# An expert's two products between the score products, and the first score of the unit behind ahead of the other steps: the order of one software-pipelined loop

## The chip, the core and the metric

The kernel runs on one core of one Trainium2 chip. The core's engines run side by side, each with its own instruction queue: TensorE (PE in the profile) multiplies matrices and writes into PSUM, VectorE (DVE) and ScalarE (ACT) read and write PSUM and SBUF, GpSimd (POOL) works on SBUF, and SyncE (SP) issues the transfers. The metric is the device time of one execution in microseconds. Three runs of the kernel before gave a median of 3007.34 us, from 3006.35 to 3009.61.

## What is computed

The reference is four blocks of attention and feed-forward network on 2048 tokens (16 sequences of 128, 256 features), each with a layer norm and a residual. The change is in the code of the last layer alone. Its attention has 16 heads of 16 features and lets every token attend to all 2048 context tokens; its feed-forward part is a mixture of eight experts, two of them weighted per token, plus a shared network of 352 hidden features:

```python
q, k, v = _fq_sym(q, axis=-1), _fq_sym(k, axis=-1), _fq_sym(v, axis=2)     # int8 grids
attn = jax.nn.softmax(jnp.einsum('bhqd,bhkd->bhqk', q, k), axis=-1)
out = jnp.einsum('bhqk,bhkd->bhqd', _fq_unsigned(attn, axis=-1), v)
...
combine = jnp.sum(jax.nn.one_hot(selected, E) * routing_weights[..., None], axis=1)   # top 2 of 8
g = jnp.einsum('nh,eih->nei', x, expert_gate)
u = jnp.einsum('nh,eih->nei', x, expert_up)
y = jnp.einsum('nei,ehi->neh', jax.nn.silu(g) * u, expert_down)
out = silu(g_sh) * u_sh @ shared_down.T + jnp.einsum('neh,ne->nh', y, combine)
```

The kernel treats the shared network as two more experts with a fixed weight, so each token passes ten experts of 176 features.

## The kernel before

**Units.** The method `l3` runs the last layer. Tokens are taken in 16 tiles of 128. A *unit* `u` is one head of one tile: tile `u // 16`, head `u % 16`; there are N = 256 units. For each unit the 128 x 2048 scores are made in four pieces of 128 x 512, each in a PSUM bank of its own: `scores` (L916, one matmul), `peak` (L922, VectorE's maximum of a piece), then `bias` (L927 and L928, two small VectorE operations over the four maxima), and `exponentials` (L938, four ScalarE activations that also sum, and one transposing transfer of the unit's result by SyncE, L942). `values` (L950, 16 small matmuls) uses the transposed result LAG = 4 units later.

**Steps.** All else in the layer is spread over the units as steps: a dictionary `steps` names, for an offset counted from the first unit of tile `t`, which functions run there. As offsets go past 16, steps of two or three tiles meet in one unit. Written by position (unit modulo 16), with the tile they serve left out:

- 0 and 1: layer norm of the next tile (`stats`, `norm`); 2 `turn_h` (two transposes on TensorE, one ScalarE copy); 3 `project_q` (four matmuls, then a VectorE addition, L984); 4 `quant_q` (three VectorE operations, then GpSimd), and `divide` (VectorE, L1017 to L1021, which frees the bank that the value products collect in); 5 `turn_o` (two transposes, two ScalarE operations); 6 `project_o` (four matmuls, then L1037 on VectorE); 7 `stats_m`, 8 `norm_m`, 9 `turn_m` (two transposes, one ScalarE copy); 10 `turn_q` (eight transposes in L1008, a ScalarE copy L1010 and a VectorE copy L1011); 11 `logits` (four small matmuls, a VectorE maximum, a ScalarE exponential L1062); 12 `top` and 13 `combine` (VectorE).
- 14, 15 and 0 to 7: one expert each, ten in all (`expert`, L1090 to L1103): four matmuls of 352 columns (two per half of the 256 features), two ScalarE activations out of that bank (L1095 `ma`, L1096 `mb`), and, as a returned function that is called later in the unit, L1099 on VectorE (`ma` times the gate half, out of the same bank), L1100 on GpSimd, and the return of the bank.
- 1, 4, 7 and 8: `turn_a` turns a part of the experts' results (four transposes, at 8 two; one ScalarE copy L973). 8, 9, 11 and 12: `down` (L1119, eight, eight, eight and four matmuls in the trace), which collects in a bank `moe` held from position 8 to 12.

**Order.** The loop is under a manual schedule: on every engine instructions run in the order in which they are written. The main part of one unit, L1156 to L1179, is:

```python
exponentials(u)
scores(u + 1, 2); peak(u + 1, 2); scores(u + 1, 3); peak(u + 1, 3)
bias(u + 1)
later = [f(t, u) for each step due]      # an expert's products and activations are in here
values(u - LAG)
scores(u + 2, 0); scores(u + 2, 1)
peak(u + 2, 0)
the functions in later                    # L1099 and L1100 of the expert
peak(u + 2, 1)
```

**Banks.** Seven PSUM banks `b0` to `b6` serve scores and steps; an eighth collects the value products. `take` (L904) gives out the free bank with the smallest number, `give` (L909) returns one with a number that says when in the unit it will be free: u + 0.2, 0.4, 0.6 and 0.8 for the four that the exponentials free, about u + 0.8 to u + 1.0 for a step's, u + 1.1 for an expert's. The choice is made when the program is built; on the chip the first instruction that writes into the bank waits for the last reader of what was in it. At the head of a unit six banks hold scores (four of `u`, two of `u + 1`), and the seventh is free or, at positions 9 to 12, holds `moe`.

Of the kernel before, what the change touches and what calls it, by code (L numbers as in the profile page):

```python
# [29 lines left out]
P = 128  # L30
NT = 16
D = 256
NH = 16
# [7 lines left out]
class Net:  # L41
# [841 lines left out]
    def l3(self, w3, moe_w):  # L883
# [7 lines left out]
        nc, tc = self.nc, self.tc  # L891
        qw, ow, qb, ob, kst, v, sv = (w3[n] for n in ("q", "o", "qb", "ob", "k", "v", "sv"))
        gate_w, wgu, wd = moe_w
        NE, IN = 10, 176
        LAG = 4
        E = mybir.EngineType
        with (tc.tile_pool(name="l3x", bufs=2) as pool, tc.tile_pool(name="l3p", bufs=3) as pp,
              tc.tile_pool(name="l3t", bufs=LAG + 1) as tp, tc.tile_pool(name="l3m", bufs=1) as mp,
              tc.tile_pool(name="l3e", bufs=3) as ep):
            st = {}  # L900
# [3 lines left out]
            def take(shape, name, dtype=F32):  # L904
                tag = min(banks, key=banks.get)
                del banks[tag]
                return self.bank(shape, tag, name, dtype), tag

            def give(tag, when):  # L909
                banks[tag] = when  # L910


            def scores(u, q):
                t, hd = divmod(u, NH)
                ps, tag = st["s", u, q] = take([P, 512], "piece")
                nc.tensor.matmul(ps, qTs[t % 2][:, hd, :],  # L916
                                 kst[q // 2][:, hd // 2, 512 * (q % 2):512 * (q % 2) + 512], start=True, stop=True)

            def peak(u, q):
                if q == 0:  # L920
                    st["nm", u] = self.s(4, "nm")
                nc.vector.tensor_reduce(st["nm", u][:, q:q + 1], st["s", u, q][0], AX.X, ALU.max, negate=True)  # L922

            def bias(u):
                t, hd = divmod(u, NH)
                nb = st["nb", u] = self.s(1, "nb")
                nc.vector.tensor_reduce(nb, st.pop(("nm", u)), AX.X, ALU.min)  # L927
                nc.vector.tensor_scalar(nb, nb, st["sq", t][:, hd:hd + 1], LN255, ALU.mult, ALU.add)  # L928

            def exponentials(u):  # L930
                t, hd = divmod(u, NH)
                if hd == 0:
                    st["z", t] = pool.tile([P, NH, 4], F32, name="z", tag="z")

                p, nb = pp.tile([P, T], I16, name="p", tag="p"), st.pop(("nb", u))
                for q in range(4):
                    ps, tag = st.pop(("s", u, q))
                    nc.scalar.activation(p[:, 512 * q:512 * q + 512], ps, AF.Exp, bias=nb,  # L938
                                         scale=st["sq", t][:, hd:hd + 1], accum_out=st["z", t][:, hd, q:q + 1])
                    give(tag, u + 0.2 * (q + 1))  # L940
                pT = st["pT", u] = tp.tile([P, NT, P], I16, name="pT", tag="pT")
                nc.sync.dma_start_transpose(pT, p)  # L942

            def values(u):
                t, hd = divmod(u, NH)
                if hd == 0:
                    st["av", t] = self.bank([P, NH, 16], "av", "av")
                pb = st.pop(("pT", u)).bitcast(F16)
                for c in range(NT):
                    nc.tensor.matmul(st["av", t][:, hd, :], pb[:, c, :], v[:, c, hd * 16:(hd + 1) * 16],  # L950
                                     start=(c == 0), stop=(c == NT - 1))
# [124 lines left out]
            def combine(t, u):  # L1076
# [10 lines left out]
                nc.gpsimd.memset(comb[:, 8:], 0.5)  # L1087
                st["comb"] = comb

            def expert(e):  # L1090
                def step(t, u):
                    ps, tag = take([P, 2 * IN], "gu")
                    self.matmul_acc(ps, [(st["mhT"][:, c, :], wgu[:, c, e, :]) for c in range(2)])
                    a, b = (ep.tile([P, IN], F32, name=n, tag=n) for n in ("ma", "mb"))
                    nc.scalar.activation(a, ps[:, :IN], AF.Tanh, scale=0.5)  # L1095
                    nc.scalar.activation(b, ps[:, IN:], AF.Identity, scale=st["comb"][:, e:e + 1])  # L1096

                    def rest():
                        nc.vector.scalar_tensor_tensor(a, a, 1.0, ps[:, :IN], ALU.add, ALU.mult)  # L1099
                        nc.gpsimd.tensor_tensor(act[:, e * IN:(e + 1) * IN], a, b, ALU.mult)  # L1100
                        give(tag, u + 1.1)
                    return rest
                return step  # L1103

            def turn_a(k):
                def step(t, u):
# [4 lines left out]
            def down(k):  # L1111
                def step(t, u):
# [7 lines left out]
                    if k == 3:  # L1120
# [6 lines left out]
            steps = {-16: [stats], -15: [norm], -14: [turn_h], -13: [project_q], -12: [quant_q], -6: [turn_q],  # L1127
                     20: [divide], 21: [turn_o], 22: [project_o],
                     23: [stats_m], 24: [norm_m], 25: [turn_m], 27: [logits], 28: [top], 29: [combine]}
            for e in range(NE):  # L1130
                steps.setdefault(30 + e, []).append(expert(e))
            for k, n in enumerate((33, 36, 39, 40)):
                steps.setdefault(n, []).append(turn_a(k))
            for k, n in enumerate((40, 41, 43, 44)):
# [2 lines left out]
            N = NT * NH  # L1137
# [4 lines left out]
            with tc.manual_schedule(engines={E.PE, E.DVE, E.Activation, E.Pool, E.SP}):  # L1142
                nc.gpsimd.memset(act[:, NE * IN:], 0.0)
                for qT in qTs:
                    nc.gpsimd.memset(qT, 0.0)
                for n in sorted(n for n in steps if n < 0):
                    for f in steps[n]:
                        f(0, -1)
                for q in range(4):
                    scores(0, q)  # L1150
                    peak(0, q)
                bias(0)
                for q in range(2):
                    scores(1, q)
                    peak(1, q)
                for u in range(N + 29):  # L1156
                    if u < N:
                        exponentials(u)
                    if u + 1 < N:
                        for q in (2, 3):  # L1160
                            scores(u + 1, q)
                            peak(u + 1, q)
                        bias(u + 1)
                    later = []
                    for t in range(NT):
                        for f in steps.get(u - NH * t, ()) if u - NH * t >= 0 or t > 0 else ():
                            later.append(f(t, u))
                    if 0 <= u - LAG < N:
                        values(u - LAG)
                    for q in range(2):  # L1170
                        if u + 2 < N:
                            scores(u + 2, q)
                    if u + 2 < N:
                        peak(u + 2, 0)
                    for f in later:
                        if f:
                            f()
                    if u + 2 < N:
                        peak(u + 2, 1)  # L1179


    def run(self):
# [79 lines left out]
```

## Time and profile before

| | |
|---|---|
| runs: median, lowest, highest | 3007.34, 3006.35, 3009.61 us |
| the profiled execution's own time | 3011.51 us |
| its span, first to last instruction | 3009.8 us |
| mean granted TensorE clock, share of full | 0.922 |
| busy over the span: PE, DVE, ACT, POOL | 82%, 65%, 58%, 33% |
| first exponential of unit 0, of unit 255 (start) | 1877.45, 2959.31 us |
| from a tile's first exponential to the next tile's, tiles 2 to 14 | 68.6 to 68.7 and 71.2 to 71.4 us in turn |

The last layer's loop takes the stretch from 1877 us to the end. Shares over the whole span mix it with three other layers, so the loop has to be read in its own stretch. The page that the profile prints has the busy time of each engine, groups of instructions by source line with the idle time ahead of them and what ended it, and transfers; further views give the same for a stretch, list who waited for whom, or put instructions in order of time. In a row of the last kind stand the start, the time from the first start to the last end of what is merged in the row, engine, line, operation, result and operands, shapes, the number of instructions, and in brackets the idle time ahead and its releaser. A TensorE row's end is modelled, and the loads of its weights stand apart as PEld.

### The profile page before, as it was taken

How to read it: one execution, taken by the hardware profiler on the slowest of the kernel's cores; microseconds unless marked ns; L12 is line 12 of the kernel's file. 1: busy time of each engine (PE TensorE's matmuls, PEld its weight loads, DVE VectorE, ACT ScalarE, POOL GpSimd, SP SyncE). 2: the span in 40 equal slices, each digit the busy share in tenths (PEclk: the TensorE clock that was granted, in tenths of full speed). 3: DMA queues.
4: the chain of work that ended last, by engine and by line, in shares of the span. 5: the costliest groups of instructions: out<-in, count | busy, mean ns of one | idle time of the engine just before them, and what ended most of it. 6: DMA issues, size and time to landing. Idle time of an engine off the chain costs nothing. (4 is left out here: it accounts for less than half of the span.)

```text
span 3009.8 us, 41685 instructions
## 1 busy us (share of the span) xinstructions
PE 2460.5 (82%) x14066; PEld 1556.2 (52%) x14066; DVE 1956.3 (65%) x5041; ACT 1755.0 (58%) x4636; POOL 1000.7 (33%) x1587
## 2 busy tenths in 40 slices
PE   4789999999999875888888885777777777777778
PEld 2456666666666543456555653344444444444445
DVE  2455666666665434566666653887788787878784
ACT  1234444444444332555555541998888888888885
POOL 2344444444443322555555541111111111112111
PEclk9899999999999887999999997589899898989999
DMA  5000000000000003000000002876666666666673
GB/s 205 1 1 1 1 1 1 1 1 1 1 1 1 1 28 102 6 3 5 5 5 4 3 1 72 154 135 123 124 117 128 121 124 121 126 122 125 118 128 62
DMA packets 559830, 171.38 MB, mean 57 GB/s; under 512 B 538912, under 2 KB 555904, under 8 KB 558848
## 3 DMA queue, kind: packets, MB, share of 16 engines
q1 hardware_dynamic: 559616, 168.72, 27.8%
q8 instruction: 111, 1.82, 0.2%
q14 instruction: 103, 0.84, 0.1%
HBM read 32.37 MB, written 2.10 MB: 11 GB/s over the span
## 5 line engine op out<-in xcount | busy, mean ns | idle before, releaser
L938 ACT ACTIVATE p<-piece,nb,hs 128x512 int16<-128x512 f32 x1024 | 785.2, 791 | 27.4 <-issue 17.0
L922 DVE TENSOR_REDUCE nm<-piece 128x1 f32<-128x512 f32 x1024 | 652.1, 684 | 107.7 <-PE piece L916 99.8
L916 PE MATMUL piece<-kst,qT 128*128 128x512 bf16 x1024 | 366.5, 414 | 200.6 <-DVE ma L1099 89.6
L1100 POOL TENSOR_TENSOR act<-ma,mb 128x176 f32<-128x176 f32 x160 | 89.0, 558 | 765.1 <-DVE ma L1099 764.7
L233 PE MATMUL gu<-w_L_ffn_wgu,mhT 128*128 128x352 f32 x640 | 252.5, 523 | 11.6 <-ACT p L938 8.0
L225 ACT COPY pT<-tp 128x512 f32<-128x512 f32 (+1 forms) x208 | 116.6, 563 | 201.6 <-PE tp L209 200.1
L916 PEld LDWEIGHTS <-qT 128*128 128x128 bf16 x1024 | 77.4, 99 | 297.2 <-issue 168.8
L938 ACT ACTIVATION_READ_ACCUMULATOR p<-piece,nb,hs 128x1 f32 x1024 | 222.2, 217 | 0.0
L259 POOL TENSOR_TENSOR kx<-kT,hmask 128x512 f32<-128x512 f32 x128 | 132.8, 1043 | 190.4 <-PE scores L262 125.4
L264 DVE TENSOR_REDUCE mx<-scores 128x4 f32<-128x512 f32 x128 | 88.2, 689 | 161.3 <-PE scores L262 161.0
L233 PEld LDWEIGHTS gu<-w_L_ffn_wgu,mhT 128*128 128x128 f32 x640 | 122.7, 205 | 131.4 <-ACT p L938 83.5
L950 PEld LDWEIGHTS <-pT 128*128 128x128 f16 x4096 | 144.7, 99 | 82.6 <-issue 68.0
L278 PEld LDWEIGHTS av<-v,pT 128*128 128x128 f32 x1024 | 136.2, 201 | 78.2 <-ACT pT L225 66.6
L233 PE MATMUL gu<-w_L_ffn_wgu,hT 128*128 128x352 f32 x512 | 173.7, 461 | 2.1 <-DVE act L432 1.6
L524 ACT ACTIVATE s<-s,nb,qs 128x128 f32<-128x128 f32 x256 | 123.2, 482 | 87.2 <-DVE nb L522 87.2
L278 PE MATMUL av<-v,pT 128*128 128x17 f32 x1024 | 136.3, 265 | 41.0 <-ACT pT L225 41.0
L269 ACT ACTIVATE p<-scores,mx,qs 128x128 f32<-128x128 f32 x256 | 96.9, 459 | 118.8 <-DVE mx L267 111.0
L950 PE MATMUL av<-v_int,pT 128*128 128x16 bf16 x4096 | 143.7, 171 | 19.6 <-DVE o L1021 19.6
L262 PE MATMUL scores<-kx,qT 128*128 128x512 f32 x256 | 153.0, 682 | 2.3 <-ACT qT L225 1.8
L539 PE MATMUL oproj<-w_L_ffn_oT,oT 128*128 128x256 f32 x512 | 128.9, 396 | 3.7 <-ACT oT L533 3.6
L1119 PE MATMUL moe<-w_L_ffn_wd,aT 128*128 128x256 f32 x448 | 127.7, 434 | 3.6 <-ACT p L938 3.6
L233 PE MATMUL q<-w_L_ffn_qT,hT 128*128 128x512 f32 x256 | 127.9, 600 | 2.1 <-DVE rot L478 2.0
(362 smaller groups left out, 5305.7 us busy)
## 6 DMA issues: line engine op xcount, KB each, us to landing
pT<-p SPq DMA_TRANSPOSE x256, 4.3
w_L_ffn_wgu<-in_L_ffn_wgu SPq DMA_DIRECT2D x1, 3520.0 KB, 11.6
w_L_ffn_wgu<-in_L_ffn_wgu SPq DMA_DIRECT2D x1, 2816.0 KB, 12.7
x<-in_x SPq DMA_DIRECT2D x16, 128.0 KB, 4.5
ctxT<-in_ctxT SPq DMA_DIRECT2D x4, 512.0 KB, 5.2
w_L_ffn_qT<-in_L_ffn_qT SPq DMA_DIRECT2D x1, 2048.0 KB, 7.9
w_L_ffn_oT<-in_L_ffn_oT SPq DMA_DIRECT2D x1, 2048.0 KB, 15.6
ctx<-in_ctx SPq DMA_DIRECT2D x16, 128.0 KB, 2.0
```

The costliest lines, as they stand in the source:

```text
L225: nc.scalar.copy(out[:, j0:j0 + m, :], ps)
L233: self.nc.tensor.matmul(ps, a, b, start=(j == 0), stop=(j == n - 1))
L259: nc.gpsimd.tensor_tensor(kx, kT[oc].unsqueeze(1).to_broadcast([P, 4, P]), self.hmask[:, hs].unsqueeze(2).to_broadcast([P, 4, P]), ALU.mult)
L262: nc.tensor.matmul(ps, qT[:, oc, :], kx, start=True, stop=True)
L278: nc.tensor.matmul(av[:, 4 * g + h, :], pT[:, h, :], v[:, 4 * g + h, :], start=True, stop=True)
L524: nc.scalar.activation(s[:, j, :], s[:, j, :], AF.Exp, bias=nb[:, j:j + 1], scale=qs[:, j:j + 1], accum_out=z[:, j:j + 1])
L539: nc.tensor.matmul(proj, oT[:, j, :], w["o"][:, c, :], start=(c == 0), stop=(c == 15))
L916: nc.tensor.matmul(ps, qTs[t % 2][:, hd, :], kst[q // 2][:, hd // 2, 512 * (q % 2):512 * (q % 2) + 512], start=True, stop=True)
L922: nc.vector.tensor_reduce(st["nm", u][:, q:q + 1], st["s", u, q][0], AX.X, ALU.max, negate=True)
L938: nc.scalar.activation(p[:, 512 * q:512 * q + 512], ps, AF.Exp, bias=nb, scale=st["sq", t][:, hd:hd + 1], accum_out=st["z", t][:, hd, q:q ...
L950: nc.tensor.matmul(st["av", t][:, hd, :], pb[:, c, :], v[:, c, hd * 16:(hd + 1) * 16], start=(c == 0), stop=(c == NT - 1))
L1119: nc.tensor.matmul(ps, st["aT", k][:r, j, :], wd[:r, c, :], start=(c == 0), stop=(c == 13))
```

## The change

An expert no longer has one function for products and activations. `expert` returns two: `product(c)`, one of the two halves of the products (the first takes the bank), and `activations(u)`, which issues the two ScalarE operations and returns the function with L1099 and L1100 as before. The experts leave the dictionary `steps` and stand in one of their own, `experts`. The loop's order changes for all units:

- between the scores (u + 1, 2) and (u + 1, 3) stands product 0 of the unit's expert, if there is one, and after (u + 1, 3) product 1;
- each peak is written right behind its score (new helper `score`);
- the score (u + 2, 0) and its peak stand behind `bias(u + 1)`, ahead of the activations, the steps and `values`;
- the score (u + 2, 1) and its peak stand at the very end, behind the functions in `later`. On TensorE, where these functions have no instruction, that is the place behind `values` as before.

The steps, their positions, the numbers given to `give` and all shapes stay as they are.

```diff
             def expert(e):
-                def step(t, u):
-                    ps, tag = take([P, 2 * IN], "gu")
-                    self.matmul_acc(ps, [(st["mhT"][:, c, :], wgu[:, c, e, :]) for c in range(2)])
+                def product(c):
+                    if c == 0:
+                        st["gu"] = take([P, 2 * IN], "gu")
+                    nc.tensor.matmul(st["gu"][0], st["mhT"][:, c, :], wgu[:, c, e, :], start=(c == 0), stop=(c == 1))
+
+                def activations(u):
+                    ps, tag = st["gu"]
                     a, b = (ep.tile([P, IN], F32, name=n, tag=n) for n in ("ma", "mb"))
...
-                return step
+                return product, activations
...
-            for e in range(NE):
-                steps.setdefault(30 + e, []).append(expert(e))
+            experts = {30 + e: expert(e) for e in range(NE)}
...
+                def score(u, q):
+                    if u < N:
+                        scores(u, q)
+                        peak(u, q)
+
                 for u in range(N + 29):
+                    now = [experts[u - NH * t] for t in range(NT) if u - NH * t in experts]
                     if u < N:
                         exponentials(u)
+                    for c in range(2):
+                        score(u + 1, 2 + c)
+                        for product, _ in now:
+                            product(c)
                     if u + 1 < N:
-                        for q in (2, 3):
-                            scores(u + 1, q)
-                            peak(u + 1, q)
                         bias(u + 1)
-                    later = []
+                    score(u + 2, 0)
+                    later = [activations(u) for _, activations in now]
                     for t in range(NT):
                         for f in steps.get(u - NH * t, ()) if u - NH * t >= 0 or t > 0 else ():
-                            later.append(f(t, u))
+                            f(t, u)
                     if 0 <= u - LAG < N:
                         values(u - LAG)
-                    for q in range(2):
-                        if u + 2 < N:
-                            scores(u + 2, q)
-                    if u + 2 < N:
-                        peak(u + 2, 0)
                     for f in later:
-                        if f:
-                            f()
-                    if u + 2 < N:
-                        peak(u + 2, 1)
+                        f()
+                    score(u + 2, 1)
```

## The prediction, made before the changed kernel ran

> **What bounds the kernel now.** I read the loop's stretch in four views: the stretch's busy times, its waits by engine, the groups of ScalarE by line, and the instructions in order of time over one tile's sixteen units. First the stretch from 1980 to 2940 us, in which nearly fourteen tiles pass in the steady pattern (columns: stretch, its length, busy time of PE, weight loads, DVE, ACT, POOL, clock, DMA):
>
> ```profile
> core 0: us, PE busy (x) PEld busy (x) DVE busy (x) ACT busy (x) POOL busy (x), PEclk, DMA share, GB/s
> 1980.00:2940.00 960.00, 746.59 (x5884) 433.53 (x5883) 765.42 (x1869) 818.71 (x2195) 165.80 (x313) 0.92 0.67 124
> ```
>
> ScalarE works 819 of 960 us, more than any other engine, and its instructions run in one fixed order. So the loop's length is ScalarE's work plus what ScalarE waits. Its waits in the same stretch, total and times:
>
> ```profile
> ACT ma L1095 <- PE gu L233: 60.6, 60, 2.2
> ACT gp L1062 <- DVE gnm L1060: 39.8, 13, 3.5
> ACT mhT L973 <- PE tp L971: 17.0, 14, 1.2
> ACT p L938 <- issue: 13.4, 13, 1.0
> ```
>
> Half of the wait is for an expert's products; the rest stands at three places without an expert. The order of time, over positions 8 to 11 of a tile (position = unit modulo 16), shows which bank each TensorE step waited for:
>
> ```profile
> 2445.52 0.81 ACT L938 ACTIVATE p<-piece,nb,hs 128x512 int16<-128x512 f32 x1
> 2445.71 1.99 PE L1119 MATMUL moe<-w_L_ffn_wd,aT 128*128 128x256 f32 x8 [0.26 <-ACT p L938]
> ...
> 2448.80 1.89 PE L1119 MATMUL moe<-w_L_ffn_wd,aT 128*128 128x256 f32 x8
> ...
> 2450.95 0.37 ACT L973 COPY mhT<-tp 128x256 f32<-128x256 f32 x1 [1.22 <-PE tp L971]
> 2451.37 0.78 ACT L938 ACTIVATE p<-piece,nb,hs 128x512 int16<-128x512 f32 x1
> ...
> 2453.65 0.78 ACT L938 ACTIVATE p<-piece,nb,hs 128x512 int16<-128x512 f32 x1
> 2453.81 0.61 PE L1008 MATMUL htp<-identb,qi 128*128 128x128 bf16 x8 [0.38 <-ACT p L938]
> ...
> 2454.45 1.01 ACT L1010 COPY qT<-htp 64x1024 bf16<-64x1024 bf16 x1
> ...
> 2457.42 3.25 PE L1119 MATMUL moe<-w_L_ffn_wd,aT 128*128 128x256 f32 x8
> ...
> 2461.25 0.27 ACT L1062 ACTIVATE gp<-logits,gnm 128x8 f32<-128x8 f32 x1 [2.75 <-DVE gnm L1060]
> ```
>
> Exponentials start every 0.76 us. With E for the start of a unit's first, TensorE gets the four banks they free at E+0.92, 1.68, 2.44 and 3.20 (first score after E=2451.37 at 2452.29, the next at 2453.05, the transposes at 2453.81). The transposes of position 10 stand on the third bank, and their copy follows the fourth exponential (2453.65 + 0.80) without a gap.
>
> [...]four gu matmuls take 1.45 us at some places and 2.55 or 2.71 at others, and tiles alternate between about 68.7 and 71.3 us. [...]here the q weight loads begin at 2423.66 and their matmuls at 2423.96. [...]here DVE's copy of qT waits for ScalarE's 15 times, 12.7 us.
>
> **The change, part by part.** Sums are per tile, relative to E, at full clock unless said. Durations: score 0.21 after the one before and 0.42 until DVE can start; one product 0.66 (half of 1.45, less the tail; +0.13 at the end); peak 0.62; bias pair 0.33; L1099 0.25 to the next; ScalarE's ma at E+3.23, mb +0.22, next unit +0.29, thus 3.74 for an expert unit without a stall.
>
> *The weave.* Which bank a step gets follows from the order of takes. Now: first score the spare bank, product pair the second freed (1.68), ready at 1.68+1.45+0.1 = 3.23, just when ma wants it: no slack. After: product 0 takes the first freed (0.92 to 1.58), the score the second (1.68), product 1 from 1.89, ready at 2.78. Slack 0.45. But the spare bank is freed by L1099 of the unit before, so this slack covers only its lateness up to about 0.8.
>
> *First score behind in front of the steps.* DVE now does this peak before a step's operations, not after. At positions 3 and 6 (q and o projections) the DVE addition waits for TensorE and today peak and L1099 stand behind it: L1099 runs at the next E+1.52 (2426.24 against 2424.72). After: q in the fourth bank 3.20 to 4.22, addition to 4.66, L1099 at once: next E+0.92. Then first score 1.31, products 1.52 to 3.18, ready 3.27 instead of 3.87. The stall of 0.64 at positions 4 and 7 goes. What is late next is their four transposes: fourth bank, after the score, 3.26 to 3.86, copy at 3.90 instead of 3.78: 0.12. Length 4.77 to 4.36: -0.41, twice.
>
> Position 5: L1099 before it sits behind 2.13 us of DVE steps of position 4 (division and quantisation). The sum on DVE is unchanged, bias to L1099; I get E+2.0 as today (1.98) and a stall of 1.1: +0.1.
>
> Positions 14 and 15: products start one bank earlier and L1099 runs about 0.4 earlier. Slow-clock gu at 14: ready 3.9 instead of 4.5, -0.55. In the other tiles, where 15 is slow: -0.5. I take -0.55.
>
> *The price.* The early score takes the bank that steps used. A step that takes a bank now gets the fourth (3.20) instead of the third (2.44). In expert units ma and mb cover it: ScalarE's copy is due at 3.74, two transposes end at 3.58; four end at 3.80, so position 1 pays 0.1. Without an expert the copy is due at 3.08, and nothing covers:
>
> - Position 8: moe gets the fourth bank, so L1119's eight matmuls start at 3.20, not 2.47. TensorE is then full until the transposes of position 9: from 2445.71 to 2450.95 it is 5.24 us, with the same number of scores in between (four). mhT comes 0.72 later; its stall goes from 1.22 to 1.95. +0.72.
> - Position 10: transposes at 3.20, end at 3.81, copy at 3.85 instead of 3.08. +0.77. The score that follows waits for DVE's half of that copy as today (next E+0.85).
> - Position 11: the score at 2.44 now stands before L1119's eight matmuls and the logits behind them. Today they start at 2.06; after, at 2.44 plus 0.21 (0.38 on slow clock): 2.65 to 2.85. +0.75, bounds 0.6 and 0.8 while their clock stays as it is.
>
> Positions 12 and 13: DVE works through from bias to bias; the sum stays, 0.
>
> Scores, products, activations, transfers and L1100 are the same in number; the transposing transfer is issued at the same place behind the exponentials and its queue passes nothing; values run four units later and stay covered. DVE's bias comes at 3.2 in an expert unit, before the next exponential at 3.74. That cover is 0.5.
>
> Sum per tile: -0.41 -0.41 -0.55 +0.1 +0.1 +0.72 +0.77 +0.75 = +1.07. Thirteen full tiles (2 to 14): 13.9. Tile 15 has no q transposes and no q projection: about +0.7. Tile 1 has a spare bank; only its logits stand behind one score more: +0.5. Units after 255 have no scores: 0. Sum +15 us. The profiled execution took 3011.5 us (span 3009.8), 4.2 over the median of the runs: 3011.5+15 = 3026.5 there, 3022 as a median.
>
> **The rivals.** *Clock against it.* [...] If each tile becomes like the long ones, 1.3 us per tile (half of 71.3-68.7) come on top: 17 us, 3039. For it: the gap on TensorE before L1119 at 11 grows by about 1.5 us. Against: two tiles now make 139.95 us, 41 windows of 3.413, and a new length locks elsewhere.
>
> *Not slower: the clock pays it back.* One mechanism: fewer half-rate windows. The long tiles lose 2.15-1.05 at position 5, 0.75 at 11 and the rest at 15 to them. If all tiles become like the short ones, -1.3 per tile meets +1.07: -3 us, 3004; it decides once the stalls at 5 and 11 no longer alternate. For it: products that start at 0.92 split the idle stretch of TensorE in an expert unit; even locking to the present length would give no change. Against: 10 and 11 get emptier.
>
> *Faster: the bank is not what the steps wait for.* If the fourth bank were ready when the third is, the losses of 2.24 at 9, 10 and 11 fall away and -1.17 per tile stays: -16 us, 2991. Against: L1119 and the transposes start within 0.2 of an exponential's release in the rows above. For it only that the three places could shift against each other. An even larger gain, all 60.6 us of ma's wait, would need position 5 without its stall, which DVE's sum denies.
>
> **How the numbers follow.** This kernel's runs tell 0.2% (6 us) from no change: below 3001.3 is faster, above 3013.4 slower. Forecast 3022, 0.48, own range 3014 to 3032 (losses of 1.9 to 2.4, gains of 1.0 to 1.6 per tile, and a locking of the length within 0.4). Clock against it 0.12. Clock pays it back 0.22, mostly within 0.2% (0.16), 0.04 faster, 0.02 slower. Bank not the limit 0.18, all faster. Faster 0.22, same 0.16, slower 0.62. The range for 8 in 10 runs from the low part of the clock case to just over the long-tile case: 2999 to 3041.
>
> **What would show it.** In the profile after: ma's wait for gu falls from 60.6 us to about 40; a new wait of the qT copy for the htp transposes, 0.77 each; mhT's wait rises from 1.22 to near 1.95 each, gp's from about 3.1 to 3.8; L1119's first eight start at the fourth exponential's release. The transposes of qT still starting at E+2.44 would refute the price; position 4 still above 4.7 us would refute the gain; ma's wait gone at position 5 would refute DVE's sum.

## The result, and the profile after

The changed kernel takes 3035.91 us (median of 4 runs, 3032.51 to 3038.6) against 3006.85 us (4 runs) of the kernel before: ratio 1.0099, 95% interval 1.008 to 1.0119. It is 29 us slower. The profiled execution took 3036.77 us, its span 3035.1 us against 3009.8. Of the 25.3 us between the two spans, 1.7 lie ahead of the loop's first exponential, where the change touches nothing, 2.1 in tiles 0 and 1, 18.7 in the thirteen tiles 2 to 14, 2.8 in tile 15, and nothing behind the last exponential.

The loop's stretch after, again nearly fourteen tiles (columns: stretch, length, busy time of PE, weight loads, DVE, ACT, POOL, clock, DMA):

```profile
core 0: us, PE busy (x) PEld busy (x) DVE busy (x) ACT busy (x) POOL busy (x), PEclk, DMA share, GB/s
1980.00:2965.00 985.00, 777.24 (x5940) 455.06 (x5940) 779.60 (x1887) 822.42 (x2213) 164.52 (x313) 0.89 0.67 121
```

ScalarE does the same work as before (822 against 819 us) in 985 instead of 960 us, and TensorE's clock is down from 0.92 to 0.89. ScalarE's waits in it:

```profile
ACT ma L1100 <- PE gu L1095: 46.0, 53, 2.3
ACT gp L1062 <- DVE gnm L1060: 44.6, 13, 3.7
ACT mhT L973 <- PE tp L971: 28.9, 14, 3.2
ACT p L938 <- issue: 23.7, 13, 2.1
ACT qT L1010 <- PE htp L1008: 9.4, 13, 1.1
ACT aT L973 <- PE tp L971: 4.5, 15, 0.3
```

The wait for the products fell by 14.6 us. All else rose: mhT by 11.9, the exponentials by 10.3, gp by 4.8, and two waits are new, qT's and aT's. Where they come from is seen in the order of time, positions 8 to 10 of a tile (L1095 is now the line of the products; behind it line numbers are five higher than before, so L1100 is L1095 of before and L1124 is L1119):

```profile
2455.13 0.79 ACT L938 ACTIVATE p<-piece,nb,hs 128x512 int16<-128x512 f32 x1
...
2456.06 1.99 PE L1124 MATMUL moe<-w_L_ffn_wd,aT 128*128 128x256 f32 x8 [0.26 <-ACT p L938]
...
2459.16 1.89 PE L1124 MATMUL moe<-w_L_ffn_wd,aT 128*128 128x256 f32 x8
...
2461.30 0.37 ACT L973 COPY mhT<-tp 128x256 f32<-128x256 f32 x1 [1.98 <-PE tp L971]
...
2461.57 0.79 ACT L938 ACTIVATE p<-piece,nb,hs 128x512 int16<-128x512 f32 x1
...
2464.02 0.38 PE L916 MATMUL piece<-kst,qT 128*128 128x512 bf16 x1 [0.38 <-ACT p L938]
...
2464.78 0.61 PE L1008 MATMUL htp<-identb,qi 128*128 128x128 bf16 x8 [0.38 <-ACT p L938]
...
2465.42 1.01 ACT L1010 COPY qT<-htp 64x1024 bf16<-64x1024 bf16 x1 [0.69 <-PE htp L1008]
```

The early score runs at 2464.02, 2.45 us after the unit's first exponential: it has the third bank. The transposes for qT run at 3.21 us, the release of the fourth, and moe's first matmuls at position 8 too (2456.06 is 0.93 after the fourth exponential's start). Each ScalarE operation behind them waits.

These waits are not yet the 29 us, for the gains stand against them. The granted clock in the two traces is either full or half. Of the half-rate stretches in their clock records, 73 before and 85 after, 38 and 54 last 3.413 us, and all others but the very last (2.10 and 1.76 us) last 2 to 18 times that; a window below is 3.413 us. In tiles 3 to 14 there are 3.5 such half-rate windows per tile before and 4.75 after. Two neighbouring tiles of the kernel before, the first with two half-rate windows (at positions 11 and 14), the second with five:

```profile
2129.18:2197.85 68.67, 52.75 (x430) 30.88 (x428) 55.55 (x136) 59.34 (x160) 12.20 (x23) 0.95 0.66 122
2197.85:2269.12 71.27, 56.08 (x430) 32.40 (x428) 55.80 (x136) 59.44 (x160) 12.24 (x23) 0.88 0.65 123
```

and two of the changed kernel, again with two (at the same positions) and with five:

```profile
2134.70:2203.24 68.54, 53.34 (x429) 31.28 (x428) 56.03 (x137) 59.05 (x160) 12.12 (x23) 0.95 0.70 125
2203.24:2274.94 71.70, 56.48 (x429) 33.27 (x428) 56.23 (x137) 59.16 (x161) 12.11 (x23) 0.88 0.67 120
```

With the same number of these windows a tile is no longer than before, or 0.4 us longer. Before, the two kinds take turns; after, of the tiles 3 to 14 all but the first of these two have five.

### The profile page after: what moved, and what is told of

Its sections match the earlier page's. It is cut to its first block, busy times and chain, and to the rows that moved or that the text cites. A ratio compares the mean times of both kernels' runs of the same rounds, so it can differ in the third digit from the quotient of the medians.

```text
span 3035.1 us, 41685 instructions
## 1 busy us (share of the span) xinstructions
PE 2490.6 (82%) x14066; PEld 1575.2 (52%) x14066; DVE 1964.9 (65%) x5041; ACT 1752.3 (58%) x4636; POOL 999.5 (33%) x1587
## 5 line engine op out<-in xcount | busy, mean ns | idle before, releaser
L922 DVE TENSOR_REDUCE nm<-piece 128x1 f32<-128x512 f32 x1024 | 670.8, 684 | 120.9 <-PE piece L916 114.6
L916 PE MATMUL piece<-kst,qT 128*128 128x512 bf16 x1024 | 404.2, 432 | 136.4 <-ACT p L938 50.7
L1095 PE MATMUL gu<-w_L_ffn_wgu,mhT 128*128 128x352 f32 x640 | 274.7, 520 | 37.5 <-ACT p L938 37.3
L916 PEld LDWEIGHTS <-qT 128*128 128x128 bf16 x1024 | 99.3, 103 | 250.2 <-issue 148.8
L1095 PEld LDWEIGHTS gu<-w_L_ffn_wgu,mhT 128*128 128x128 f32 x640 | 124.9, 208 | 128.3 <-ACT p L938 73.5
L1124 PE MATMUL moe<-w_L_ffn_wd,aT 128*128 128x256 f32 x448 | 137.6, 459 | 3.4 <-ACT p L938 3.4
```

Source lines behind the costliest of these rows:

```text
L916: nc.tensor.matmul(ps, qTs[t % 2][:, hd, :], kst[q // 2][:, hd // 2, 512 * (q % 2):512 * (q % 2) + 512], start=True, stop=True)
L1095: nc.tensor.matmul(st["gu"][0], st["mhT"][:, c, :], wgu[:, c, e, :], start=(c == 0), stop=(c == 1))
L1124: nc.tensor.matmul(ps, st["aT", k][:r, j, :], wd[:r, c, :], start=(c == 0), stop=(c == 13))
```

## The experiments

Theory A: the early score costs, since it takes the third freed bank and leaves a step the fourth; the weave gains. Rival B: the weave, or what it does to TensorE's clock, costs, and the banks don't matter. All changes below are made to the changed kernel unless said. Lengths of a position are the distance from a unit's first exponential to the next unit's, means over tiles 3 to 14, read off ScalarE's instructions in order of time:

| position | before | after | difference forecast | measured | weave alone | early score in expert units only |
|---|---|---|---|---|---|---|
| 0 | 3.73 | 3.51 | 0 | -0.22 | 3.55 | 3.51 |
| 1 | 4.20 | 4.52 | +0.1 | +0.32 | 4.11 | 4.50 |
| 2 | 4.01 | 3.95 | 0 | -0.06 | 3.77 | 3.95 |
| 3 and 4 | 8.55 | 8.08 | -0.41 | -0.47 | 8.17 | 8.08 |
| 5 | 5.76 | 6.22 | +0.1 | +0.46 | 5.65 | 5.98 |
| 6 and 7 | 8.52 | 8.13 | -0.41 | -0.39 | 8.10 | 8.14 |
| 9 | 4.84 | 5.53 | +0.72 | +0.69 | 4.84 | 5.22 |
| 10 | 3.99 | 4.79 | +0.77 | +0.80 | 3.99 | 3.99 |
| 11 | 6.50 | 6.89 | +0.75 | +0.39 | 5.28 | 5.26 |
| 13 | 4.18 | 5.04 | 0 | +0.86 | 4.17 | 4.17 |
| 14 and 15 | 9.10 | 8.16 | -0.55 | -0.94 | 8.31 | 8.10 |
| whole tile | 69.97 | 71.41 | +1.07 | +1.44 | 66.55 | 67.50 |
| half-rate windows in it | 3.5 | 4.75 | | +1.25 | 1.8 | 2.4 |

(Positions 8 and 12 stay at 3.29 and 3.30.)

**The weave alone.**

```diff
-                    score(u + 2, 0)
                     later = [activations(u) for _, activations in now]
...
+                    for q in range(2):
+                        if u + 2 < N:
+                            scores(u + 2, q)
+                    if u + 2 < N:
+                        peak(u + 2, 0)
                     for f in later:
                         f()
-                    score(u + 2, 1)
+                    if u + 2 < N:
+                        peak(u + 2, 1)
```

> The weave alone; the first score of the unit behind goes back behind the values, so the steps get the third bank again. Theory A (the early score costs, because steps get the fourth bank; the weave gains): positions 8 to 13 return to the lengths of before (9: 4.84, 10: 3.99, 11: 6.1 to 6.9, 13: 4.18 us), expert units without a step keep 3.51; positions 4 and 7 return to about 4.77. Some 1.5 us per tile under the kernel before: about 2986 us. Rival B (the weave is what costs, through TensorE's clock): stays near 3036 us.

Measured: 2970.46 us (4 runs), ratio to before 0.9869, interval 0.9853 to 0.9885. Its ScalarE waits over a like number of tiles:

```profile
ACT ma L1100 <- PE gu L1095: 44.2, 54, 2.8
ACT gp L1062 <- DVE gnm L1060: 23.7, 13, 3.5
ACT mhT L973 <- PE tp L971: 15.8, 13, 1.2
ACT p L938 <- issue: 13.3, 13, 1.0
```

mhT's, qT's and the exponentials' waits are those of before; the products' wait is as low as in the changed kernel. Rival B falls: the weave gains, more than theory A forecast, since gp's wait fell too (position 11 at 4.6 in most tiles), although nothing there was changed. That is the clock: it is at 0.932, and a tile has 1.8 half-rate windows instead of 3.5.

**The early score alone**, with both products behind it.

```diff
                     for c in range(2):
                         score(u + 1, 2 + c)
-                        for product, _ in now:
-                            product(c)
...
                     score(u + 2, 0)
+                    for product, _ in now:
+                        for c in range(2):
+                            product(c)
```

> The early score alone, products together behind it. Theory A: the products now get the bank of the third exponential (2.44 us after the unit's first), are ready at 4.0 and ma, due at 3.0, waits 1.0 us in each of the ten expert units, on top of the losses at 8 to 13: some 10 us per tile over the weave's, about 3125 us. Rival B: without the weave near 3007 us, as before.

Measured: 3159.98 us (6 runs), ratio 1.0494, 1.0476 to 1.0512. The products' wait is 0.84 us in each of the ten expert units where the clock is up and mostly about 2.1 where it is down. A tile has 8.4 half-rate windows, and what the products' wait exceeds 0.84 us by comes to 71 us in tiles 2 to 14 of the profiled execution (3174.89 us, clock 0.885, one of the slower ones). So the slow clock is more than enough for the miss of 35 us. The 0.84 us is the price of the third bank, paid ten times a tile.

**The early score in expert units only.**

```diff
-                    score(u + 2, 0)
+                    early = bool(now)
+                    if early:
+                        score(u + 2, 0)
```

(otherwise the order at the end is that of before)

> Weave, and the early score only in units with an expert; positions 8 to 13 in the old order. Theory A: 8 to 13 as before, experts as in the changed kernel: 67.2 us per tile with a full clock at positions 5 and 11, 69.2 with a slow one, against 69.98 before and 71.68 after: 2970 to 2996 us. Rival B: the order at 8 to 13 is not what costs, near 3036 us.

Measured: 2981.34 us (4 runs), ratio 0.9905, 0.9888 to 0.9921. So the early score at the positions without an expert costs 3035.9 - 2981.3 = 54.6 us. In expert units it costs 2981.3 - 2970.5 = 10.9 us more than the weave alone: positions 1 and 2 grow by 0.4 and 0.2, for the copies now wait for the fourth bank, and 3, 4, 6 and 7 gain 0.05 in sum. Another 0.4 at position 9 and 0.3 at position 5 are slow clock: 9 is 4.82 us in nine of the twelve tiles and about 6.4 in three, where a half-rate window falls on 8 and 9.

**Position 12 alone in the old order.**

```diff
+                    early = u % NH != 12
```

(the rest as in the run before this one)

> The changed kernel with the old order at position 12 alone. Theory A: moe's last four matmuls start at 1.9 instead of 2.8 us, VectorE's addition behind them no longer waits 0.95, and the gap ahead of position 14 falls from 2.06 to 1.03 us; positions 9 to 11 stay at 5.43, 4.76 and 7.0. If the clock's pattern stays, 1.03 per tile less: 3022 us. Rival B: no gain at 14, near 3036 us.

Measured: 3013.02 us (20 runs), ratio 1.0015, 1.0007 to 1.0024. The gap ahead of position 14 is back at 1.02 us in every tile. In the changed kernel the order of time there is:

```profile
2475.78 0.58 PE L916 MATMUL piece<-kst,qT 128*128 128x512 bf16 x1 [0.38 <-ACT p L938]
...
2476.16 1.91 PE L1124 MATMUL moe<-w_L_ffn_wd,aT 128*128 128x256 f32 x4
...
2478.11 0.42 DVE L1126 TENSOR_TENSOR x<-moe,x 128x256 f32<-128x256 f32 x1 [0.95 <-PE moe L1124]
...
2481.87 0.78 ACT L938 ACTIVATE p<-piece,nb,hs 128x512 int16<-128x512 f32 x1 [2.06 <-issue]
```

moe's last four matmuls stand behind the early score and run at half rate, 1.91 us instead of 1.03; VectorE, which works without a break up to the next bias, waits 0.95 for them, and the exponential of position 14 is that much later. The order alone doesn't do it: tiles 2 to 4 of the changed kernel have the same order but no half-rate window there, the four matmuls take 1.03 us, and position 13 is 4.17 us as before. In this run no such window falls on position 12, so it doesn't tell whether the old order would have covered slow matmuls. The gain of 23 us is more than this term alone (0.86 x 13 = 11): the slow clock at positions 5 and 11 went in part as well.

**Position 10 alone in the old order**, the same edit with 10 for 12.

> The changed kernel with the old order at position 10 alone. Theory A: the copy of qT no longer waits, position 10 falls from 4.76 to 3.99 us, and position 9 stays at 5.43; by this term alone 10 us, 3026 us, and more or less where the clock's windows fall otherwise. If qT's wait is not from the order at this position: 4.76 us stays.

Measured: 3002.41 us (20 runs), ratio 0.9997, 0.9985 to 1.0009. Position 10 is back at 4.00 to 4.14 us in tiles 2 to 13, 9 stays at 5.43 in all but one. The term is confirmed; the time fell by 33 us where the term is worth 10. Undoing either position also takes half-rate windows away (3.25 per tile with the old order at 12, 3.8 here, 4.75 in the changed kernel), so these two times don't price the terms. The lengths do, in tiles with the same windows.

**More work for TensorE at positions 10 to 13**, in the changed kernel and in the kernel before: the value products are made again, into the same place.

```diff
                     if 0 <= u - LAG < N:
-                        values(u - LAG)
+                        pb = st["pT", u - LAG]
+                        for _ in range({10: 3, 11: 2, 12: 3, 13: 3}.get(u % NH, 1)):
+                            st["pT", u - LAG] = pb
+                            values(u - LAG)
```

> The changed kernel, with the value products of positions 10, 12 and 13 made three times and of 11 twice into the same place, so that TensorE has more to do where it is emptiest; the result stays. If this keeps the clock up, position 11 falls from 7.0 to about 5.0 us, the gap ahead of 14 from 2.06 to 1.03, and 5 may fall from 6.4 to 5.2, while 9 (5.43) and 10 (4.76), which theory A puts down to the banks alone, stay: 67 to 68 us per tile, 2970 to 2986 us. If the clock is only a consequence and not a cost, or the extra work doesn't reach it: near 3036 us.

> The kernel before with the same extra value products. With the clock up: position 11 from 6.1 and 6.9 to 4.6 us, 14 and 15 to 4.2 and 3.7, 5 at 5.2: 66.4 us per tile, about 2957 us. What the change costs without the clock is then the difference to the other run of this kind: theory A, banks and order alone, some +0.5 us per tile (+7 us); if the clock was the only cost, 0.

Measured: 2999.59 us (20 runs), 0.9979 (0.9969 to 0.9989), for the changed kernel; 2986.98 us (5 runs), 0.9939 (0.9918 to 0.996), for the one before. Both gain from work that nothing needs, so the clock is a cost. It is not the only one: positions 9 and 10 stay at 5.43 and 4.76, and the changed kernel stays behind, by 0.4% instead of 1.0% (0.9979 over 0.9939; the two intervals above don't overlap). The separation isn't clean: one half-rate window per tile is left in most tiles of either kernel, in the changed one at 11, which stayed at 6.2, in the one before at position 5 (6.8 us in most tiles). The clock is not quite the same (0.933 to 0.938 in the runs of the changed kernel, 0.936 to 0.941 in those of the one before), so the 0.4% may have clock in it too. And the profiled executions don't stand for the medians, 2989.52 us being 10 below and 2998.38 us 11 above theirs: in them the last tiles are 68.26 and 68.23 us long, all but equal.

**L1099 ahead of VectorE's steps**, on the weave alone.

```diff
+                            if f in (project_q, project_o, quant_q):
+                                while later:
+                                    later.pop(0)()
                             f(t, u)
```

> The weave alone, and L1099 of the expert ahead of the q and o additions (positions 3 and 6) and ahead of the quantisation (4) on VectorE, so that the spare bank comes free earlier. If the stalls at 4, 7 and 5 are the late L1099: position 4 from 4.63 to 4.0, 7 from 4.59 to 4.0, 5 from 5.42 to about 4.5 us, some 2 us per tile, 2942 us. If they are something else: 2970 us as with the weave alone.

Measured: 2949.05 us (4 runs), ratio 0.9809, 0.9782 to 0.9836: the fastest kernel here but for the next, whose interval overlaps it. Position 4 is 4.10, 5 is 4.83, 7 is 4.01, so the stalls there were L1099's lateness. ScalarE's wait for the products fell from 44.2 to

```profile
ACT ma L1100 <- PE gu L1095: 14.4, 15, 1.0
ACT ma L1100 <- POOL q L997: 5.6, 13, 0.5
```

The second line is what is left at position 5, put down to GpSimd. The prediction held that the sum of VectorE's work there denies the unit without its stall; the sum is the same here, and only the order was in the way.

**The two together.**

> The weave with L1099 ahead of the VectorE steps, and the extra value products at positions 10 to 13. If the rest of position 11's and 14's wait is the slow clock: 11 from 5.68 to 4.62, 14 from 4.66 to 4.2, against 0.28 lost at 12: some 1.2 us per tile, about 2932 us. If slow windows only move elsewhere (to position 5 as in the kernel before with the same extra products): no gain, 2949 us.

Measured: 2946.31 us (4 runs), ratio 0.9789, 0.977 to 0.9809: no gain that can be told. Position 11 fell to 5.47 only, 14 to 4.60, and 12 lost 0.28. Nearly every tile has two half-rate windows in both, at 11 and 14: the extra products didn't take them away here.

**Are the tiles held to whole windows?** In the changed kernel the last ten tiles before the sixteenth are 71.68 to 71.70 us each, where 21 windows of 3.413 us, the length in the clock records, make 71.67; the same ten of the two kernels just told are 64.78 to 64.86, and 19 windows make 64.85. An unused ScalarE copy was added at position 2 of the kernel with L1099 first, once and three times.

```diff
                 st["hT"] = turn(st["h"], 2, "hT", pool, u)
+                if t > 0:
+                    for _ in range(1):
+                        extra = mp.tile([P, D], F32, name="extra", tag="extra")
+                        nc.scalar.copy(extra, st["h"])
```

> The weave with L1099 first (64.85 us per tile in its last tiles, which is 19 times 3.413), with one more ScalarE copy of 128 x 256 at position 2 whose result nothing reads: 0.25 us more of the engine that sets the length. If the tiles are held to whole windows of the clock: 64.85 stays and another position's slow-clock wait gives 0.25 back, 2949 us. If not: 65.1 us per tile, +3.5 us, 2953 us.

> The same with three such copies, 0.75 us per tile. Not held: 65.6 us per tile, +10 us, 2959 us. Held: 64.85 as long as the slow-clock waits (about 1.1 at position 11, 0.45 at 14) can give it back, or a jump to another whole or half number of windows (66.55 or 68.27 us per tile, 2972 or 2995 us).

Measured: 2955.9 us (4 runs), 0.9826 (0.981 to 0.9843), and 2963.5 us (4 runs), 0.9872 (0.9845 to 0.9899). One copy lengthened position 2 by 0.31 and was not held: tiles went to 63.9 to 66.0 us. Three lengthened it by 1.26, and yet ten of the thirteen tiles took 64.84 to 65.29, since position 11 gave back 1.06; tiles 7 to 9 slipped to 66.8 to 68.9. That execution was the fastest of its four (2960.57 us). The medians show nothing held: against the 2949.05 us without copies they are 6.9 and 14.5 us longer (5 and 19 by the ratios to the kernel before), where the copies' own length makes 5 and 19 in the fifteen tiles that have them. So a tile's length can stay at whole windows for ten tiles on end, but added work isn't given back for it.

## Why the prediction was right, and which terms were off

The forecast was 3022 us, slower, in a range of 2999 to 3041. The direction and the waits at positions 9 and 10 came as it said. The size came in part by luck: it put the +1.07 per tile down to banks and order with the clock as it was, and in tiles with the same half-rate windows little of that sum is there (-0.14 us with two, +0.4 with five). What made the kernel slower is that nearly all its tiles have five such windows. With the two kinds in turn, as before, its own lengths of 68.54 and 71.68 would make 70.11 us, +0.14 per tile in place of +1.44. That is an estimate; its 68.54 rests on one tile here and on four (68.54 to 68.63) in the run with the old order at 12. By the prediction's own steps:

- *Positions 9 and 10*: +0.72 and +0.77 forecast, +0.69 and +0.80 measured (with some slow-clock tiles in it; 0.59 and 0.77 where the pattern is regular). Confirmed, also by the old order at 10.
- *Position 11*: +0.75 forecast, +0.39 measured. moe's matmuls start 2.82 us after E, inside the 2.65 to 2.85 given; but the term held only "while their clock stays", and it didn't: in the tile with two half-rate windows they start 0.76 later than before and take 2.42 instead of 3.23 us, as the window has gone by sooner (it begins 0.47 us after E, before 1.29 to 1.39), and the position is 6.08 us against 6.10 to 6.15. The +0.39 is the larger share of five-window tiles. Position 11 at a full clock throughout is in no tile of the changed kernel.
- *Positions 12 and 13, "the sum stays, 0"*: the term that failed. It left out a wait of VectorE for moe's four matmuls. At full rate, 1.03 us, there is none, as tiles 2 to 4 show. They ran at half rate in the other ten: +0.86 per tile, 11 us in all. The prediction had the slow clock as a rival of its own (3039 us), but gave it no place here.
- *The weave*: the -0.55 for positions 14 and 15 is right in tiles with two half-rate windows (8.17 for 8.74 us, -0.57). The -0.94 of the table has the five-window tiles in it, where before two of the windows lay there and now one does. And "no slack" at the plain expert units was wrong: 3.74 us was not a unit without a stall. There was a hidden wait of 0.22 for the products in it, as units 0, 3, 6 and 15 show.
- *Positions 4 and 7*: the size is right if each is taken with its neighbour ahead (-0.47 and -0.39 for -0.41), the cause isn't. The prediction gave the gain to the early score; the weave alone brings nearly all of it (8.17 and 8.10), and the early score next to nothing.
- *Position 5*: "+0.1" measured +0.46, all of it slow clock: 5.16 us where the clock is up, against 5.23 before.
- *The early score's whole price* was taken at 2.24 us per tile in units without an expert, some 30 us; it is 54.6 us in the runs, with the half-rate windows that it brings. The gains in expert units were taken at -1.17 per tile, 16 us; the run with the early score in these units only gains 26.8 us (3008.1 before in those runs, minus 2981.3), and the weave alone 37.6. Both sides were too small, and in a sum of opposite signs nearly half of the miss cancelled.
- *Tiles 1 and 15* were given +0.5 and +0.7 us; they are 1.85 and 2.78 longer.

Of the three rivals, "clock against it" was nearest in time, and it is the larger part: it said that each tile becomes like the long ones, and eleven of the thirteen did. The two kernels with extra work put it at somewhat more than half of the 29 us, though they don't separate it cleanly; the estimate from the tiles puts it at some 17 of the 18.7 us in tiles 2 to 14. But the main sum was not to be added to it in full, as the rival had it. "The bank is not what the steps wait for" falls with the transposes at E+3.21. Not settled is how much of the 54.6 us is bank order by itself and how much the slow windows that it brings, nor why they come: the experiments show that the early score brings them and the weave takes them away, not by which gap on TensorE. The four lengths 9, 10, 11 and 13 come to 2.74 us, 36 to 38 us over thirteen or fourteen tiles, the rest is at 5, 14 and in tiles 1 and 15.

## What to carry to other kernels

When an instruction is moved ahead in a loop that hands out buffers in order, list what it takes from the instructions that it passes, and which of these have no cover; here ScalarE's two activations covered most of the later bank in expert units, and nothing did elsewhere (the early score costs 10.9 us there, 54.6 at the other positions). Try the parts of a change apart: one half of this one gains 1.3%, and the other takes 2.2% on top of it. And a unit's length without a reported wait is not yet its length without a stall; take it from an engine's rate. Where the clock changes in the loop, compare stretches with the same number of slow windows before an order is priced.

## What the runs showed of the hardware that was not expected

A wait can hide where one engine's instructions overlap in the trace. An activation whose input is long there starts 0.76 us after the start of the exponential ahead of it, which lasts 0.80; in the changed kernel (order of time, position 15):

```profile
2488.78 0.80 ACT L938 ACTIVATE p<-piece,nb,hs 128x512 int16<-128x512 f32 x1
...
2489.54 0.34 ACT L1100 ACTIVATE ma<-gu 128x176 f32<-128x176 f32 x1
```

In the kernel before, the same pair starts 0.96 apart, at 2411.28 and 2412.24, and the view shows no idle time there; the unit is 0.22 us longer all the same. What it waits for are the products:

```profile
2410.70 1.45 PE L233 MATMUL gu<-w_L_ffn_wgu,mhT 128*128 128x352 f32 x4
```

They end at 2412.15 by the trace, 0.87 after the exponential's start; in the changed kernel they are done before ScalarE comes to them.

TensorE's half-rate windows come back at the same places in tile after tile, and in some kernels the tile's length settles near a whole number of windows: 71.68, 68.26, 64.85 us are 21, 20 and 19 times 3.413 (the changed kernel, that with extra value products, that with L1099 first); in the kernel before two tiles together make 139.95, 41 windows. In others, as that with one extra copy, it doesn't settle (63.9 to 66.0 us). Where terms of 0.86 and 0.77 us in a tile, some 10 us in all, were taken away, half-rate windows went with them (from 4.75 per tile to 3.25 and 3.8), and the time fell by 23 and 33 us.

Two of the prediction's rivals count gaps on TensorE for or against half-rate windows. That was its author's estimate; that a gap brings them is not shown. In tiles 2 to 14 of the kernel before, with two or five half-rate windows each, TensorE never idles longer than 1.52 us, in those of the changed kernel, with two to five, never longer than 2.31. In the 32 full-rate windows ahead of a half-rate one it is, in the kernel before, busy for 33 to 58% of the time, in the 189 ahead of another full-rate one for 56 to 100%, by the trace's modelled ends of the matmuls.
